# A four-layer graph network: own values summed by TensorE in the first convolution, first columns of the search placed ahead, and the last chunk of the edge stage divided

## The chip, the cores and the metric

The kernel runs on one core of one Trainium2 chip. A core has TensorE (PE, matrix multiplication, with a separate record for the loading of weights, PEld), VectorE (DVE), ScalarE (ACT), GpSimd (POOL, which here issues the indirect gathers) and SyncE (SP, which here issues the plain DMAs). [...] The metric is the device time of one execution in microseconds, median over runs.

## The reference, cut to what matters

A graph of 6250 nodes with 64 features and 206,250 directed edges (every edge both ways, and a loop at each node), sorted by destination. Four residual layers, each on the normalised and clipped values:

```python
h = jnp.maximum(_layernorm(x, axis=-1), 0.0)
x = x + _L0_gnn_ref(h, edge_index, W3, b3, W4, b4)      # two convolutions, A + an extra loop
h = jnp.maximum(_layernorm(x, axis=-1), 0.0)
x = x + _L1_gnn_ref(h, edge_index)                      # one pass of the normalised A
h = jnp.maximum(_layernorm(x, axis=-1), 0.0)
x = x + _L2_gnn_ref(h, edge_attr_64, src, dst, ...)     # an edge network, mean of squares by node
h = jnp.maximum(_layernorm(x, axis=-1), 0.0)
x = x + _L3_gnn_ref(edge_index, h)                      # three passes, mean of four embeddings
...
# _L0: y = D^-1/2 (A + I) D^-1/2 x, then W and b; a relu between the two
# _L2: msg = sigmoid(x @ Bw + Bb) * Vp[src] + (x @ Cw + Cb); M = clip(msg, EPS)^2, mean over dst, root
# _L3: embs = A (norm[row] * norm[col] * embs), three times; (emb + embs1 + embs2 + embs3) / 4
```

The self loop that the convolution adds on top of the loops of the graph is the `+ I` of L0: each node's own value is added to what it gathers. In the last layer, the first of the three passes needs the output of the edge layer at every node.

## The kernel before, in words

**Layout.** Nodes are padded to 49 blocks of 128 (6272). Seven chunks of seven blocks (`CB`) are 896 nodes (`W`); fourteen strips of 448 nodes (`CW`). The kernel builds the dense matrix of edge counts, A, in fp8, strip by strip of 448 columns, and stores it in DRAM as seven arrays of 128 x 49 x 896; all passes are then matmuls with that matrix. fp32 node values are split into three bf16 parts that add up to them (`split`, L709 to L715: ACT rounds, DVE subtracts, ACT rounds, DVE subtracts) and kept as `U3` or `V3`: 128 nodes x 49 blocks x 3 parts x 64 features. A pass multiplies all three parts. There are two forms of it. In `spread` (L742 to L750) the values are the weights and the matrix the moving operand, 448 wide: features come out on the partitions, with the parts going to two halves that are added when turned to nodes (`to_nodes`, L735 to L740, seven fp32 matmuls with a doubled identity `twice`). In `gather` (L1002 to L1031) pieces of the matrix (784 KB, 7 x 7 blocks) are the weights and the values move, 192 wide (3 parts x 64): an output chunk takes 343 matmuls in four PSUM banks `p_acc`, opened by four matmuls with a tile of zeros; four DVE reduces add the three parts, and the function `then` takes the chunk on.

**Stage 1, 0 to 166 us.** Inputs, the normalised values H0, and a search for where each block of 256 matrix columns begins in the edge list. For 25 columns DVE counts in a table `near` how many entries lie below the column's start (L801 to L804); one scaling (L805) and one conversion to integers (L806) follow for all 25, and POOL then gathers for each column, with these as indices, a stretch of the list (`near2`, L869) and with a second, exact index the run of edges (`run`, L878). The first strip is built here; degrees and U3 follow.

**Stage 2, to 563 us.** Fourteen strips; each has fourteen steps of `build` (DVE compares two digits with a count, L849; PE multiplies, L858; ACT writes the strip, L862). Beside the building of one strip `convolve` multiplies the one before (`spread` for 49 blocks, in fourteen stretches), and `hidden` takes a whole chunk through the two dense layers of L0: it turns the sum to nodes, copies it (ACT, L951), adds the three parts of the own values with three DVE adds (`add_whole`, L717 to L723), scales it (L954), multiplies, and splits the result into V3.

**Stages 3 and 4, to 1058 us.** Two gathers, for the second convolution (`convolved`; the seventh chunk's `hidden` and the constants of the edge stage, `prepared`, are taken in steps between its pieces) and for L1 (`turned`).

**Stage 5, to 3662 us: edges.** 202 groups of 1024 edges go through 208 slots as a pipeline seven slots deep (`slot`, an order written out by hand for PE, ACT and DVE). In each slot one group is fetched (eight indirect DMAs of POOL, L1325), others are in the edge network, gated (L1356, L1360 to L1362), squared and summed to nodes. When the groups of a chunk of nodes are through, `finished` (L1293 to L1304) takes the root, adds to X, normalises and splits the chunk into the U3 of the last layer. Beside that, a list `todo` is worked off, some items in each slot. It holds loads of pieces (SP, L1226), comparisons of A with its transpose that verify the edge list (`crossed`: PE turns four or three blocks, L1234, DVE compares, L1240), and the parts of the first pass of the last layer (`partial`: for chunk i, once it is finished, its 21 matmuls of 448 for one strip, L1252, which DVE adds to `Y`, L1258). The planner takes in slot i the number of open items divided by the slots left to the next deadline; the deadlines `ends` (L1308, L1315) are the slots in which the seven chunks end: 35, 64, 93, 122, 151, 180, 207. The last chunk ends with the last slot, so its part of the first pass is left for the next stage.

**Stage 6, to the end: three passes of L3.** In the first (L1498 to L1511) the last chunk's part is done: seven pieces, fourteen strips of 21 matmuls, DVE adds each to `Y` (L1509), and for every second strip `to_nodes` and `propagated` (L1477 to L1495: scale, scale again, `split` into the next pass's V3, and add to H). The second and third passes are gathers. PE, DVE and ACT have no order written out by hand here; the second pass's first matmul comes after the first pass's last. The functions touched stand below, with the lines of the profile.

Of the kernel before, what the change touches and what calls it, by code (L numbers as in the profile page):

```python
# [16 lines left out]
P = 128  # L17
# [578 lines left out]
QN = 32  # L596
DRIFT = 32
# [19 lines left out]
def fast(ctx, tc, bad, x, src, dst, edge_attr, W3, b3, W4, b4, w1, b1, w2, b2, Bw, Bb, Cw, Cb,  # L617
# [47 lines left out]

    node = ctx.enter_context(tc.tile_pool(name="node", bufs=1, reuse_waits="tile"))
# [24 lines left out]
    def normed(h, X_c):  # L691

        m = stat.tile([P, CB], F32, name="m")
        nc.vector.tensor_reduce(m, X_c, axis=AX.X, op=OP.add)
        nc.vector.tensor_scalar_mul(m, m, 1.0 / D)
        nc.vector.tensor_sub(h, X_c, over_features(m))
        q = stat.tile([P, CB, D], F32, name="q")
        nc.vector.tensor_mul(q, h, h)
        v = stat.tile([P, CB], F32, name="v")
# [3 lines left out]
        nc.vector.scalar_tensor_tensor(h, h, 0.0, over_features(v), op0=OP.max, op1=OP.mult)  # L703
# [4 lines left out]

    def split(u, U3, c):  # L709
        u3 = U3[:, blocks(c), :, :]  # L710
        nc.scalar.activation(u3[:, :, 0, :], u, AF.Copy)
        r = stat.tile([P, CB, D], F32, name="r")
        nc.vector.tensor_sub(r, u, u3[:, :, 0, :])
        nc.scalar.activation(u3[:, :, 1, :], r, AF.Copy)
        nc.vector.tensor_sub(u3[:, :, 2, :], r, u3[:, :, 1, :])  # L715
# [40 lines left out]
    with ExitStack() as ph:  # L756
# [44 lines left out]
        for c in range(GC):  # L801
            w = min(max(int(c * 2 * P * E / N / LOOK) - 22, 0), NS - SW)
            nc.vector.tensor_scalar(junk, near[:, w:w + SW], start_of[:, c:c + 1], float(w - 1),
                                    op0=OP.is_lt, op1=OP.add, accum_out=begin[:, c:c + 1])  # L804
        nc.vector.tensor_scalar(begin, begin, float(LOOK), 0.0, op0=OP.mult, op1=OP.max)  # L805
        nc.vector.tensor_copy(begin_i, begin)  # L806
# [20 lines left out]
        with ExitStack() as ps:  # L827
# [101 lines left out]
            for c in range(NC):  # L929
                u = wpool.tile([P, CB, D], F32, name="z", bufs=2)  # L930
                nc.vector.tensor_mul(u, H0[:, blocks(c), :], over_features(norm0[:, blocks(c)]))
                split(u, U3, c)
# [4 lines left out]
            def convolve(s, strip):  # L937

                p = psum.tile([P, 512], F32, name="p_sum", bufs=2)
                for q in range(NQ):  # L940
                    for b in range(q * NB // NQ, (q + 1) * NB // NQ):
                        spread(p, U3, b, strip[:, b, :], CW)
# [5 lines left out]
            def hidden(c, wpool, psum):  # L948

                z = wpool.tile([P, CB, D], F32, name="z", bufs=2)  # L950
                nc.scalar.activation(z, to_nodes(psum, y[c], CB), AF.Copy)  # L951
                yield
                add_whole(z, U3, c)
                nc.vector.tensor_mul(z, z, over_features(norm0[:, blocks(c)]))  # L954
# [16 lines left out]
                split(u, V3, c)  # L971
# [24 lines left out]
    def normed_and_split(h, U3, c, scale):  # L996
        normed(h, X[:, blocks(c), :])
        u = stat.tile([P, CB, D], F32, name="u")
        nc.vector.tensor_mul(u, h, over_features(scale[:, blocks(c)]))
        split(u, U3, c)  # L1000
# [554 lines left out]
```

## Time and profile before

| what | value |
| --- | --- |
| median of three runs | 4117.7 us (4096.95 to 4123.5) |
| profiled execution | 4134.23 us, span 4132.5 us |
| PE busy | 3161.0 us, 76% |
| DVE busy | 1984.4 us, 48% |
| ACT busy | 1257.3 us, 30% |
| POOL busy | 1663.9 us, 40% |
| edge stage | 1058 to 3662 us, granted TensorE clock 0.78 |
| rest of the first pass | 3673 to 3718 us |
| two later passes | 14 chunks of 28.95 us |

The page's groups name a line, an engine, an operation, the tiles written and read, and the count; after the bar stand the busy time, the mean duration of one in ns, and the idle time of the engine ahead of it with what ended that. Matmuls are pipelined and their ends are modelled, so a busy PE need not be at its peak. The waits name the engine and line that waited, what released it, the total, the number of times and the longest.

### The profile page before, as it was taken

To read this page: it belongs to the slowest core of one execution; us is meant where nothing else is said; L and a number is where in the kernel's file an instruction comes from. 1 tells how busy PE (TensorE), PEld (TensorE's weight loads), DVE (VectorE), ACT (ScalarE), POOL (GpSimd) and SP (SyncE) were. 2 spreads that over 40 slices of the span, in tenths; PEclk is the share of its full clock that TensorE was granted. 3 is DMA by queue.
4 is the path that set the end of the run, shared out by engine and by line. 5 is a ranking of instruction groups with operands and counts; after the bars stand their busy time and mean duration, and the time that the engine had idled before them with its cause. 6 is when DMAs were issued, how large, how long until landed. Compare 5 with 4: busy or idle time off the path is not lost.

```text
span 4132.5 us, 59248 instructions
## 1 busy us (share of the span) xinstructions
PE 3161.0 (76%) x24225; PEld 2164.1 (52%) x24225; DVE 1984.4 (48%) x3916; ACT 1257.3 (30%) x2031; POOL 1663.9 (40%) x1889
## 2 busy tenths in 40 slices
PE   1799999999566667676677667767767766689999
PEld 0566679998233334343334333334433433349999
DVE  6999945322245445454545443545544444461111
ACT  1577730000233333333333233333333333320000
POOL 4100010000566666656566656566666655600000
PEclk9799999999677767778787877777878777889999
DMA  3234355653322222222222222222222222136664
GB/s 99 74 83 109 85 167 188 204 179 117 97 66 60 46 56 72 56 82 56 65 66 64 62 66 62 65 63 60 81 57 73 68 53 68 45 106 194 196 203 151
DMA packets 229311, 388.75 MB, mean 94 GB/s; under 512 B 137573, under 2 KB 139743, under 8 KB 228771
## 3 DMA queue, kind: packets, MB, share of 16 engines
q1 hardware_dynamic: 170420, 321.51, 24.7%
q0 software_dynamic: 55104, 60.65, 7.7%
q8 instruction: 192, 3.15, 0.3%
q10 hardware_dynamic: 3504, 2.70, 0.3%
q14 instruction: 91, 0.75, 0.1%
HBM read 340.47 MB, written 44.24 MB: 93 GB/s over the span
## 4 chain that ended last, share of the span: by engine, by line
PE 51%; DVE 16%; another core or an unknown queue 13%; issue 9%; ACT 7%; DMA 2%; POOL 1%; DVEq 0%; SPq 0%; ACTq 0%; POOLq 0%
PE p_acc L1017 18%; PE p_sum L748 9%; PE p_bc L1351 7%; PE p L1337 5%; PE p_a L858 3%; DVE junk L1240 2%; ACT h L1341 2%; PE p_s L1379 2%; DVE m L1361 2%; DVE m L1360 2%; PE p_bc L1347 2%; PE p_e L1333 2%; DVE m L1362 1%; ACT gate L1356 1%
## 5 line engine op out<-in xcount | busy, mean ns | idle before, releaser
L1325 POOL DMA_INDIRECT v<-Vp_dram,src_g x1616 | 1590.6, 984 | 1348.6 <-issue 818.9
L1017 PE MATMUL p_acc<-U,piece 128*128 128x192 bf16 x9604 | 818.1, 246 | 3.6 <-DMA piece<-A 3.6
L1017 PEld LDWEIGHTS <-piece 128*128 128x128 fp8e4 x9604 | 799.1, 98 | 15.8 <-issue 4.7
L1351 PE MATMUL p_bc<-BC,h 128*128 128x256 f32 x1616 | 572.9, 486 | 6.9 <-issue 6.3
L1234 PE MATMUL p_sum<-ident_b,piece 128*128 128x128 bf16 x1372 | 160.1, 240 | 369.6 <-DVE junk L1240 325.2
L1360 DVE TENSOR_TENSOR m<-gate,v 128x512 f32<-128x512 f32 x202 | 140.1, 693 | 626.9 <-ACT gate L1356 417.4
L1240 DVE SCALAR_TENSOR_TENSOR junk<-p_sum,there 128x512 bf16<-128x512 f32 (+1 forms) x392 | 242.0, 617 | 394.7 <-remote 307.5
L1351 PEld LDWEIGHTS p_bc<-BC,h 128*128 128x128 f32 x1616 | 336.0, 231 | 163.4 <-issue 127.2
L1234 PEld LDWEIGHTS <-piece 128*128 128x128 fp8e4 x1372 | 120.6, 109 | 527.0 <-issue 505.6
L748 PEld LDWEIGHTS <-U 128*64 128x64 bf16 x4116 | 234.3, 113 | 303.5 <-issue 167.2
L862 ACT ACTIVATE strip<-p_a 128x784 fp8e4<-128x784 f32 x392 | 302.0, 820 | 118.6 <-PE p_a L858 102.6
L748 PE MATMUL p_sum<-piece,U 128*64 128x448 fp8e4 x2058 | 272.4, 384 | 80.9 <-issue 59.6
L1337 PE MATMUL p<-h,w_d 128*128 128x512 f32 x404 | 270.0, 752 | 73.6 <-ACT h L1341 58.8
L1027 DVE TENSOR_REDUCE zg<-p_acc 128x128 f32<-128x384 f32 x112 | 56.9, 508 | 534.8 <-PE p_acc L1017 534.1
L1341 ACT ACTIVATE h<-p,b_c 128x512 f32<-128x512 f32 x404 | 261.3, 685 | 169.0 <-remote 80.6
L1424 ACT ACTIVATE m<-m 128x512 bf16<-128x512 f32 x202 | 127.3, 630 | 594.0 <-DVE m L1423 468.6
L1379 PE MATMUL p_s<-m,to 128*128 128x192 bf16 x1616 | 207.0, 276 | 117.9 <-DVE r_s L1387 61.7
L1347 PE MATMUL p_bc<-BC_b,ones 3*128 3x512 bf16 x404 | 181.9, 450 | 118.8 <-DVE m L1361 105.3
L1337 PE MATMUL p<-eT,w_d 128*128 128x512 f32 x404 | 250.2, 705 | 17.7 <-issue 8.1
L1367 ACT ACTIVATE m<-m 128x512 bf16<-128x512 f32 x202 | 127.2, 630 | 431.0 <-DVE m L1362 342.8
L1379 PEld LDWEIGHTS <-to 128*128 128x128 bf16 x1616 | 174.1, 150 | 145.3 <-issue 141.3
L1347 PEld LDWEIGHTS <-ones 3*128 3x128 bf16 x404 | 37.5, 93 | 399.5 <-issue 208.2
(198 smaller groups left out, 3488.8 us busy)
## 6 DMA issues: line engine op xcount, KB each, us to landing
piece<-A SPq DMA_DIRECT2D x249, 784.0 KB
e<-in_edge_attr SPq DMA_DIRECT2D x202, 256.0 KB
A<-strip SPq DMA_DIRECT2D x14, 2744.0 KB
v<-Vp_dram,src_g POOLq DMA_INDIRECT x1616
there<-A SPq DMA_DIRECT2D x28, 784.0 KB
pairs<-pair SPq DMA_DIRECT2D x1, 1616.0 KB
Vp_dram<-v SPq DMA_DIRECT2D x7, 224.0 KB
out<-X SPq DMA_DIRECT2D x6, 224.0 KB
```

The source lines that it names most:

```text
L748: nc.tensor.matmul(p[half * D:(half + 1) * D, :w], U3[:, b, k, :], at_block, start=(i < 2), stop=(i >= 3 * n - 2))
L862: nc.scalar.activation(strips[s][:, :, col:col + 2 * SG].rearrange("p b (j l) -> p b j l", l=2), p[:, :, :2 * NB].rearrange("p j (b l) -> ...
L1017: nc.tensor.matmul(p[d // 2][:, d % 2 * 3 * D:(d % 2 + 1) * 3 * D], t[:, b, d * P:(d + 1) * P], U3[:, k * CB + b, :, :].rearrange("p t f - ...
L1234: nc.tensor.matmul(p[:, a - a0, :], held["here"][:, a, b * P:(b + 1) * P], ident_b, start=True, stop=True)
L1240: nc.vector.scalar_tensor_tensor(junk[:, :(a1 - a0) * P], p[:, :a1 - a0, :].rearrange("p a q -> p (a q)"), 15.5, there, op0=OP.min, op1=OP ...
L1325: nc.gpsimd.indirect_dma_start(out=v[:, j, :], out_offset=None, in_=Vp_dram[:, :], in_offset=bass.IndirectOffsetOnAxis(ap=src_g[:, g, j:j ...
L1337: nc.tensor.matmul(of[g][p], w, of[g].pop(x), start=True, stop=True)
L1341: nc.scalar.activation(of[g][t], of[g].pop(p), **how)
L1347: nc.tensor.matmul(p_bc[:, 4 * b:4 * b + 4].rearrange("p j o f -> p (j o f)"), ones, BC_b, start=True, stop=False)
L1351: nc.tensor.matmul(p_bc[:, 2 * q:2 * q + 2].rearrange("p j o f -> p (j o f)"), h2[:, q * P:(q + 1) * P], BC, start=False, stop=(k == 1))
L1360: nc.vector.tensor_mul(m, of[g].pop("gate"), of[g].pop("v"))
L1379: nc.tensor.matmul(p, to[:, :, j], m3[:, j].rearrange("p t f -> p (t f)"), start=(j == 0), stop=(j == J - 1))
```

## The change

Five edits.

1. In the search the 25 columns go in three groups (0 to 2, 3 to 9, 10 to 24); each group's scaling and conversion follow its own columns.
2. In `convolve` PE adds the own values: ahead of the last block's matmuls of a strip, twelve matmuls take U3's parts of the strip's own nodes with columns of the identity into the same bank. `hidden` then has no copy and no `add_whole`: the scaling reads PSUM.
3. The tile of zeros is made once, ahead of everything, and `gather` has a parameter for the steps taken beside it.
4. The edge stage knows eight parts in place of seven chunks (`PARTS`): the last chunk is divided in its first four blocks and its last three (`LATE`). The deadlines are 35, 64, 93, 122, 151, 180, 196 and 207. When the four blocks are finished, their loads (seven, of 448 KB) and sums (fourteen, of 12 matmuls) are put on the list, and between them `by_node` turns each finished chunk of `Y` to nodes (seven matmuls, and a copy to `Yn`).
5. The last three blocks' part of the first pass is in the gather's form: seven chunks of 21 matmuls of 192 columns in four banks `p_late`, four reduces, the addition of `Yn`, and `propagated`. It is a generator, `rest_of_first`: two chunks go ahead, and the others between the pieces of the second pass's first output chunk. The order of PE and DVE in this stage is now as written.

```diff
-        for c in range(GC):
...
-        nc.vector.tensor_scalar(begin, begin, float(LOOK), 0.0, op0=OP.mult, op1=OP.max)
-        nc.vector.tensor_copy(begin_i, begin)
+        for c0, c1 in ((0, 3), (3, 10), (10, GC)):
+            for c in range(c0, c1):
...
+            nc.vector.tensor_scalar(begin[:, c0:c1], begin[:, c0:c1], float(LOOK), 0.0,
+                                    op0=OP.mult, op1=OP.max)
+            nc.vector.tensor_copy(begin_i[:, c0:c1], begin[:, c0:c1])
...
                     for b in range(q * NB // NQ, (q + 1) * NB // NQ):
+                        if b == NB - 1:
+                            for d in range(s * CW // P, -(-(s + 1) * CW // P)):
+                                lo_, hi_ = max(d * P, s * CW), min((d + 1) * P, (s + 1) * CW)
+                                for k in range(3):
+                                    nc.tensor.matmul(
+                                        p[k % 2 * D:(k % 2 + 1) * D, lo_ - s * CW:hi_ - s * CW],
+                                        U3[:, d, k, :], ident_b[:, lo_ - d * P:hi_ - d * P],
+                                        start=False, stop=False)
                         spread(p, U3, b, strip[:, b, :], CW)
...
-                nc.scalar.activation(z, to_nodes(psum, y[c], CB), AF.Copy)
-                yield
-                add_whole(z, U3, c)
-                nc.vector.tensor_mul(z, z, over_features(norm0[:, blocks(c)]))
+                nc.vector.tensor_mul(z, to_nodes(psum, y[c], CB),
+                                     over_features(norm0[:, blocks(c)]))
...
+        PARTS = [(c * CB, CB) for c in range(NC - 1)] + [(NB - CB, CB - LATE), (NB - LATE, LATE)]
...
+        def by_node(k):
+
+            p = ps_a.tile([P, 512], F32, name="p_sum", bufs=2)[:, :CB * D].rearrange(
+                "p (b f) -> p b f", f=D)
+            y = Y[:, 2 * k:2 * k + 2, :].rearrange("p s w -> p (s w)")
+            for b in range(CB):
+                nc.tensor.matmul(p[:, b, :], y[:, b * P:(b + 1) * P], twice, start=True, stop=True)
+
+            def copied():
+                nc.vector.tensor_copy(Yn[:, blocks(k), :], p)
+
+            return copied
...
-            if c < NC - 1:
-                plan(CROSS[c], True)
+            if part < NC - 1:
+                plan(CROSS[part], True)
+            elif part == NC - 1:
+                for k in range(NC):
+                    todo.append((piece, lo, n, k))
+                    todo.append((partial, part, 2 * k))
+                    if k:
+                        todo.append((by_node, k - 1))
+                    todo.append((partial, part, 2 * k + 1))
+                todo.append((by_node, NC - 1))
...
-        ends = [last[c * CB + CB - 1] for c in range(NC)]
+        ends = [last[lo + n - 1] for lo, n in PARTS]
...
-                for s in range(CS):
-                    if s % 2 == 0:
-                        whole = apool.tile([P, CB, W], COUNT, name="piece")
-                        nc.sync.dma_start(whole, A[s // 2][:, blocks(NC - 1), :])
-                    t = whole[:, :, s % 2 * CW:(s % 2 + 1) * CW]
-                    p = psum.tile([P, 512], F32, name="p_sum", bufs=2)
-                    for b in range(CB):
-                        spread(p, U3, NB - CB + b, t[:, b, :], CW, NB - CB, CB)
-                    nc.vector.tensor_add(Y[:, s, :], Y[:, s, :], p[:, :CW])
-                    if s % 2:
-                        propagated(s // 2, to_nodes(
-                            psum, Y[:, s - 1:s + 1, :].rearrange("p s w -> p (s w)"), CB))
...
+        def rest_of_first():
+
+            for c in range(NC):
+                t = apool.tile([P, LATE, W], COUNT, name="late", bufs=NC)
+                nc.sync.dma_start(t, A[c][:, NB - LATE:, :])
+                p = [psum.tile([P, 512], F32, name=f"p_late{q}") for q in range(4)]
+                for d in range(CB):
+                    for b in range(LATE):
+                        nc.tensor.matmul(
+                            p[d // 2][:, d % 2 * 3 * D:(d % 2 + 1) * 3 * D],
+                            t[:, b, d * P:(d + 1) * P],
+                            U3[:, NB - LATE + b, :, :].rearrange("p t f -> p (t f)"),
+                            start=(b == 0), stop=(b == LATE - 1))
+                z = wpool.tile([P, CB, D], F32, name="zg")
+                summed_parts(z, p)
+                nc.vector.tensor_add(z, z, Yn[:, blocks(c), :])
+                propagated(c, z, V3)
+                yield
+
+        with tc.manual_schedule(engines={ET.PE, ET.DVE}):
+            rest = rest_of_first()
+            next(rest)
+            next(rest)
+            gather(apool, wpool, psum, V3, to_last, rest)
+            gather(apool, wpool, psum, values[0], to_out)
```

The diff's remaining lines give `normed`, `split` and `normed_and_split` a stretch of blocks in place of a chunk's number, and move the reduces of `gather` into `summed_parts`.

## The prediction

> **What bounds the kernel now.** I read the share of each engine by stage first. The columns are length, PE, weight load, DVE, ACT and POOL busy, granted TensorE clock, DMA share and GB/s. The stages in order: the strips of A, the edge stage, the step from it to the last passes, the rest of the first pass, and the first output chunk of the second pass.
>
> ```profile
> 166.00:563.00 397.00, 394.62 (x4899) 255.91 (x4901) 381.99 (x408) 294.93 (x409) 0.05 (x1) 1.00 0.32 87
> 1058.00:3662.00 2604.00, 1802.77 (x8343) 1000.06 (x8343) 1224.32 (x2713) 866.26 (x1448) 1580.99 (x1606) 0.78 0.25 65
> 3662.00:3674.00 12.00, 3.84 (x26) 1.71 (x24) 9.12 (x21) 2.03 (x4) 0.00 (x0) 0.73 0.01 1
> 3674.00:3718.00 44.00, 44.00 (x383) 27.71 (x380) 26.52 (x45) 6.92 (x12) 0.00 (x0) 0.96 0.35 111
> 3718.00:3748.00 30.00, 30.00 (x359) 29.68 (x358) 4.76 (x9) 1.15 (x2) 0.00 (x0) 1.00 0.59 189
> ```
>
> The reader sees three regimes: two full engines in the strips, no full engine in the edge stage (63% of the span), and PE alone from 3674 on. The groups of the strips, by shape, tell which of PE and DVE leads there:
>
> ```profile
> L849 DVE TENSOR_TENSOR lo<-count,key 128x2048 bf16<-128x2048 bf16 x172 | 209.6, 1219 | 0.0
> L849 DVE TENSOR_TENSOR hd<-turns,key 128x1568 bf16<-128x1568 bf16 x171 | 165.7, 969 | 8.1 <-PE p_a L858 7.3
> L858 PEld LDWEIGHTS <-lo 128*128 128x128 bf16 x2752 | 134.1, 98 | 65.2 <-DVE lo L849 44.8 <-issue 11.9 <-DVE hd L849 4.2
> L723 DVE TENSOR_TENSOR z<-z,r 128x448 f32<-128x448 f32 x6 | 3.7, 618 | 0.8 <-ACT z L951 0.8
> ```
>
> PE's weight loads wait 49 us for DVE, DVE waits 7 us for PE: DVE leads. In the edge stage the waits are a circle:
>
> ```profile
> POOL v L1325 <- DVE m L1360: 503.1, 91, 13.9
> ACT m L1424 <- DVE m L1423: 468.6, 141, 18.3
> PE p_sum L1234 <- DVE junk L1240: 325.2, 90, 13.0
> ```
>
> POOL's gathers of v, eight at about 1.25 us, fill 10 us of a mean slot of 12.74 us. Last, the tail from 3663 to 3748:
>
> ```profile
> L748 PE MATMUL p_sum<-piece,U 128*64 128x448 fp8e4 x304 | 35.9, 372 | 8.2 <-ACT U L711 7.4 <-ACT U L714 0.7
> L739 PE MATMUL p_node<-twice,Y 128*128 128x64 f32 x98 | 13.8, 281 | 0.0
> L1509 DVE TENSOR_TENSOR Y<-Y,p_sum 128x448 f32<-128x448 f32 x14 | 8.7, 619 | 5.5 <-PE p_sum L748 5.1
> L713 DVE TENSOR_TENSOR r<-u,U 128x448 f32<-128x448 f32 x8 | 5.0, 625 | 1.5 <-ACT U L711 0.8
> L714 ACT ACTIVATE U<-r 128x448 bf16<-128x448 f32 x8 | 4.6, 577 | 5.5 <-DVE r L713 5.5
> L1027 DVE TENSOR_REDUCE zg<-p_acc 128x128 f32<-128x384 f32 (+1 forms) x4 | 2.0, 508 | 23.0 <-PE p_acc L1017 23.0
> ```
>
> PE waits 8 us for U3 and is then never idle. The start of the program is a chain, whose POOL waits for begin_i:
>
> ```profile
> L869 POOL DMA_INDIRECT near<-pairs,begin_i x25 | 26.6, 1065 | 51.9 <-DVE begin_i L806 44.0 <-issue 6.1 <-DVE exact_i L875 0.6
> ```
>
> [...] granted clock 0.5 from 3667.5 to 3677.7, after the wait for U3. [...] An output chunk of the later passes takes 28.95 us for 347 matmuls here, 83.4 each.
>
> **The change, part by part.**
>
> *First columns ahead.* The near gather (L869) starts at 48.58, after the scale and cast (0.18 each) of all 25 columns. Placing three columns first would let it start near 40.3. But in the order of the changed program the first gather's wait is still on the count of the last column's search: its tile takes the space of the searched one, which must be read to the end. It saves two small operations ahead of the wait and adds four: 4 x 0.18 - 0.36, **+0.3**. If the wait were on the first group alone: -3.7.
>
> *Own values by TensorE.* For each of six chunks in the strips DVE loses three adds (0.610 + 0.616 + 0.618 = 1.84 us), ACT a copy (0.55); the scaling reads PSUM instead. Two strips take 62.9 us, of which 28 builds are 57.1, so what DVE drops is nearly all time: about 1.6 x 6 = -9.7. PE gains 12 matmuls of up to 128 columns for each strip[...], hidden by PE's slack of 0.36 us for each build (14 in a strip). The last strip's stand before the first piece of gather 1, which waits for its DMA until 580.67 though p_sum ended at 576.85. I take **-8**; ends: -11 (all DVE time) and +6 (PE leads[...]). The zeros tile made once: nothing on the path.
>
> *Edge stage.* Planned items are spread over slots, with a deadline when a chunk ends. The six block-row chunks before keep their deadlines. The last is divided: its first four blocks end in slot 196, three in 207. So the planned work of slots 181 to 207 (about three items in each) is now in 181 to 196 (five). An item's price: the mean slot is 12.09 us in the first chunk (1.55 crossings in each slot) and 12.90 in the sixth (1.93 crossings, 0.48 sums). That and a fit over all slots bracket 0.4 to 0.64 for a crossing and 0.93 to 1.84 for a sum of 21 matmuls. Added: 14 sums of 12 matmuls (12/21 of 0.96, 0.55) and 7 turns to nodes (0.6). Eight sums of 21 leave the last five slots (26 us, PE-led: 8 x 2.27 = 18.2 us); 5 small sums and 3 turns (9.2 us) take their place: I take -7 of the 9, as the slot's own chain is late next. Earlier slots get those eight (8 x 0.93 = 7.4) and the other nine sums and four turns (7.4). Finishing four blocks amid the stage: the five slots that finish a chunk take 18.8 us, six over the mean; with smaller operations 5. Sum 7.4 + 7.4 - 7 + 5 = **+13**. [...] Crowding therefore goes up to +45. Below zero: -8, where circle waits (POOL's 503 us) swallow the items and only the lighter last slots count.
>
> *Step to the last passes.* From the last slot to U3 is 11.1 us (3662.5 to 3673.6); 15 operations shrink from 448 to 192 columns: [...]**-3.7**. A last copy to Yn: **+0.6**.
>
> *Rest of the first pass.* Before: PE starts 3673.0, the second pass's first chunk ends 3747.67, 74.6 us. Removed: 14 x 21 matmuls of 448 columns (2.2 us a strip), 49 turns and the 14 Y adds. Added: seven chunks of 21 matmuls of 192 columns (21 x 83.4 ns = 1.75 us), between pieces (49 x 83.4 = 4.1). PE's step is 5.85 us. DVE's chain for a chunk, in the written order: four reduces 2.0, Yn 0.62, z 0.64, u 0.62, wait for ACT 0.73, r 0.63, wait 0.64, U 0.62, H 0.62: 7.15. A piece waits for its chunk's U, so **DVE becomes the bound**: the first late bank 0.5, seven chains 50, the last piece 4.1 and its tail 1: 55.6, so -19. The first matmuls are at half clock: +1.5. **-17.5**; ends -27 (PE's 5.85 a step) and -10 (chain 8 us). Late pieces are 336 KB, seven of them with seven whole ones are 7.8 MB in 55 us, 143 GB/s, under the 189 of the later passes. Later passes keep their work.
>
> Sum: 0.3 - 8 + 13 - 3.7 + 0.6 - 17.5 = **-15.3**. Against the profiled execution (4134.23 around a span of 4132.5) that is 4119; it lies 16.5 above the median of the runs shown, so from 4117.7 I get **4102**.
>
> **Rivals.**
> - *Crowding (slower).* Slots 181 to 196 hold five items and feed SP's queue; if the bound there is the items' own chain, each grows by 2 to 4 us, the stage by 30 to 60. From +28 on the whole is slower than before; at +45 it gives 4134. For it: slots of 25 us recur where crossings are three to a slot. Against: mean slots barely follow the items.
> - *PE-bound tail.* DVE's chain overlaps more than I allow, and the items are free: -8 - 3.1 - 27 + 3 = -35, 4083. Against: two ACT waits stand in the written order.
> - *No effect ahead.* The columns placed first do not start POOL earlier: that is in my forecast; were it otherwise, 4099.
> - *Strips turn PE-bound.* +6 in place of -8: 4116. For it: PE is shown 99% busy, though its ends are modelled.
>
> **How the numbers follow.** Forecast and its neighbour 4099: 0.52. Strips: 0.13. PE-bound tail: 0.17. Crowding: 0.18. About 1%, 41 us, is what a measurement of this kernel can tell (the three runs spread by 26.5). Faster than 4076.5 needs the tail and more: 0.1. Slower than 4159 needs crowding beyond +70: 0.09. Range: 4076 to 4140, from the PE-bound tail with some spread to crowding at +45 with the runs' own spread.
>
> **What would show it.** POOL's first gather still near 48.9; two strips in 61.2 us; the sixth chunk's slots 181 to 196 about 14 us; first late matmul about 8 us after the last slot; seven DVE chains 7.1 us apart with PE waiting for U between pieces; the second pass's first chunk ending 56 us after that matmul. Wrong if slots 181 to 196 pass 16 us, or if PE never waits there.

## The result and the profile after

The changed kernel takes 4122.9 us (median of 20 runs), the kernel before 4119.98 (20 runs): ratio 0.9996, 95% interval 0.9976 to 1.0015. Nothing has moved that can be measured. The ratio rests on the fast runs alone (one of the changed kernel's twenty, 4164.44 us, is counted as slow), so it is not the quotient of the two medians. The forecast was 15 us less.

The two profiled executions are 24 us apart (4110.15 against 4134.23), and that must not be read as the result: runs of one kernel spread over 60 to 77 us, and in the traces nearly all of the spread is in the edge stage. What repeats from trace to trace is the rest of the program. So I read the two traces by part, and for the edge stage take three traces of each kernel (the second and third come from the experiments, same kernels, with slots of the same length):

| part | predicted | measured | from |
| --- | --- | --- | --- |
| start and strips, to the start of the last build | -7.7 | +2.6, +3.0, +3.3 | 559.2 to 561.8; 559.7 to 562.7; 559.3 to 562.6 |
| edge stage, its last 25 slots (from slot 180 to 205) | +13 | +23 | 317.8, 315.5, 307.6 before; 327.1, 346.2, 337.1 after |
| from the last addition of edges to the first reduce of the second pass | -20.6 | -26.8 | 84.6, 84.7, 85.0 before; 57.8, 57.7, 58.3 after |

Between the second row and the third, up to the last addition of edges, another 1 to 2 us go. The sum is about +1, and the measured ratio says -1.6 (-10 to +6). The 176 earlier slots of the edge stage hold the same items in both kernels and differ only by their spread (2215 to 2250 us before, 2233 to 2262 after). So a saving of 27 us in the tail is there, the strips lost 3 in place of giving 8, and the end of the edge stage gave the rest back.

**Strips.** Groups by shape in the strips, after:

```profile
L856 DVE TENSOR_TENSOR lo<-count,key 128x2048 bf16<-128x2048 bf16 x172 | 209.0, 1215 | 0.0
L856 DVE TENSOR_TENSOR hd<-turns,key 128x1568 bf16<-128x1568 bf16 x171 | 165.2, 966 | 19.4 <-PE p_a L865 17.9
L865 PEld LDWEIGHTS <-lo 128*128 128x128 bf16 x2736 | 133.6, 98 | 59.7 <-DVE lo L856 37.0 <-issue 14.6 <-DVE hd L856 4.7
```

The three adds are gone, and DVE's idle time ahead of hd has grown from 8.1 to 19.4 us: the 11 us that were freed became a wait for PE. Why is seen when the stage is cut at its strips and not averaged. First a strip without dense layers beside it, then one with them (the columns are those of the stages in the prediction); before:

```profile
309.70:338.00 28.30, 27.98 (x374) 17.90 (x370) 28.30 (x29) 21.98 (x30) 0.00 (x0) 1.00 0.37 101
338.00:372.60 34.60, 34.56 (x417) 22.75 (x413) 32.50 (x36) 25.29 (x37) 0.00 (x0) 1.00 0.31 83
```

and after:

```profile
310.30:338.60 28.30, 28.30 (x383) 18.45 (x380) 28.30 (x29) 21.86 (x30) 0.00 (x0) 1.00 0.37 101
338.60:373.70 35.10, 34.89 (x431) 23.36 (x428) 31.05 (x33) 24.91 (x36) 0.00 (x0) 1.00 0.30 82
```

A plain strip is VectorE's: 28.30 busy of 28.30. A strip with the dense layers was PE's already before: VectorE has 32.50 busy of 34.60, PE 34.56. The change takes VectorE's work out of just these strips (31.05 busy now) and puts matmuls into them: 35.1.

**Edge stage.** Waits, after:

```profile
POOL v L1368 <- DVE m L1403: 524.5, 94, 15.7
ACT m L1468 <- DVE m L1467: 438.4, 134, 20.6
DVE junk L1260 <- remote: 287.0, 39, 17.7
```

The same circle as before ("remote" is a releaser that the profile cannot name; the kernel before has 307.5 us of it at its comparisons too). The planned work is where the prediction put it: in slots 181 to 196 PE starts 916 matmuls, 645 before. The last 25 slots take 13.5 us each in place of 12.5. A finer cut tells more: slots 181 to 196 take 225.7, 234.7 and 235.3 us (205.5, 198.7 and 208.2 before), and from there to the last addition of edges it is 89.2, 90.5 and 92.2 (100.1, 95.0 and 87.2 before). The crowded slots lost 28 us, and the lighter ones behind them gave back 3 or 4.

**Tail.** One chunk of VectorE's chain, the second of the seven, in order of time:

```profile
3679.47 1.74 DVE L1019 TENSOR_REDUCE zg<-p_late 128x128 f32<-128x384 f32 x4
3681.24 0.62 DVE L1564 TENSOR_TENSOR zg<-zg,Yn 128x448 f32<-128x448 f32 x1
3681.90 0.62 DVE L1524 TENSOR_TENSOR z<-zg,norm 128x448 f32<-128x448 f32 x1
3682.56 0.62 DVE L1527 TENSOR_TENSOR u<-z,norm 128x448 f32<-128x448 f32 x1
3683.83 0.62 DVE L717 TENSOR_TENSOR r<-u,U 128x448 f32<-128x448 f32 x1 [0.64 <-ACT U L715]
3685.09 0.62 DVE L719 TENSOR_TENSOR U<-r,U 128x448 bf16<-128x448 f32 x1 [0.64 <-ACT U L718]
3685.64 0.62 DVE L1530 TENSOR_TENSOR H<-H,z 128x448 f32<-128x448 f32 x1
3686.17 1.74 DVE L1019 TENSOR_REDUCE zg<-p_late 128x128 f32<-128x384 f32 x4
```

The chain takes 6.70 us (3679.47 to 3686.17), with both waits for ScalarE in it (the first chunk takes 7.8, waiting for PE at its reduces), and PE waits for it, as the groups from 3658 to 3735 show:

```profile
L1037 PE MATMUL p_acc<-U,piece 128*128 128x192 bf16 x477 | 41.6, 246 | 9.0 <-DVE U L719 9.0
L1557 PE MATMUL p_late<-U,late 128*128 128x192 bf16 x147 | 14.7, 263 | 5.3 <-DVE U L719 5.3
```

**Start.** POOL still waits for the end of the search. The releaser shown is now the scaling of the last group, which ends at 48.00 us, and no longer begin_i:

```profile
L876 POOL DMA_INDIRECT near<-pairs,begin_i x25 | 26.0, 1042 | 51.9 <-DVE begin L811 43.5 <-issue 5.5 <-DVE digits L889 1.6
```

The first gather starts at 48.09 us (48.58 before).

### The profile page after: what moved, and what is told of

Its sections match the earlier page's. It is cut to its first block, busy times and chain, and to the rows that moved or that the text cites. A ratio compares the mean times of both kernels' runs of the same rounds, so it can differ in the third digit from the quotient of the medians.

```text
span 4108.0 us, 59675 instructions
## 1 busy us (share of the span) xinstructions
PE 3144.2 (77%) x24414; PEld 2172.4 (53%) x24414; DVE 1995.9 (49%) x3952; ACT 1257.5 (31%) x2030; POOL 1659.2 (40%) x1889
## 4 chain that ended last, share of the span: by engine, by line
PE 52%; DVE 16%; another core or an unknown queue 12%; issue 9%; ACT 7%; DMA 2%; POOL 0%; DVEq 0%; ACTq 0%; SPq 0%; POOLq 0%
PE p_acc L1037 17%; PE p_sum L752 10%; PE p_bc L1394 7%; PE p L1380 5%; PE p_a L865 4%; ACT h L1384 2%; PE p_s L1422 2%; DVE junk L1260 2%; DVE m L1404 2%; DVE m L1403 2%; PE p_bc L1390 2%; PE p_e L1376 1%; PE p_sum L1254 1%; DVE m L1405 1%
## 5 line engine op out<-in xcount | busy, mean ns | idle before, releaser
L1368 POOL DMA_INDIRECT v<-Vp_dram,src_g x1616 | 1586.0, 981 | 1368.8 <-DVE m L1403 524.5
L1394 PE MATMUL p_bc<-BC,h 128*128 128x256 f32 x1616 | 562.9, 478 | 14.2 <-issue 13.6
L752 PEld LDWEIGHTS <-U 128*64 128x64 bf16 x3990 | 234.1, 115 | 337.1 <-issue 208.1
L1380 PE MATMUL p<-h,w_d 128*128 128x512 f32 x404 | 260.3, 727 | 68.8 <-ACT h L1384 50.7
L1422 PE MATMUL p_s<-m,to 128*128 128x192 bf16 x1616 | 206.2, 276 | 90.5 <-DVE r_s L1430 44.0
L1380 PE MATMUL p<-eT,w_d 128*128 128x512 f32 x404 | 243.6, 687 | 14.6 <-ACT h L1384 10.4
L752 PE MATMUL p_sum<-strip,U 128*64 128x448 fp8e4 x2058 | 242.1, 359 | 2.5 <-ACT U L715 1.4
```

What stands on the lines that cost most here:

```text
L752: nc.tensor.matmul(p[half * D:(half + 1) * D, :w], U3[:, b, k, :], at_block, start=(i < 2), stop=(i >= 3 * n - 2))
L1368: nc.gpsimd.indirect_dma_start(out=v[:, j, :], out_offset=None, in_=Vp_dram[:, :], in_offset=bass.IndirectOffsetOnAxis(ap=src_g[:, g, j:j ...
L1380: nc.tensor.matmul(of[g][p], w, of[g].pop(x), start=True, stop=True)
L1394: nc.tensor.matmul(p_bc[:, 2 * q:2 * q + 2].rearrange("p j o f -> p (j o f)"), h2[:, q * P:(q + 1) * P], BC, start=False, stop=(k == 1))
L1422: nc.tensor.matmul(p, to[:, :, j], m3[:, j].rearrange("p t f -> p (t f)"), start=(j == 0), stop=(j == J - 1))
```

## The experiments

The experiments fell on three chips. On one of them the kernel before takes 4092 to 4182 us, with one run of 4215, much as in the result. On the two others it takes 3616, some 500 us less, and the traces put some 490 of these into the edge stage: 2065 to 2083 us from its first to its last comparison of nodes in the kernels traced there, 10.3 a slot, against 2523 to 2609 and 12.6 to 13.0. I call the first a long-slot chip and the others short-slot chips. The waits of the edge stage on a short-slot chip, in the kernel h_early below:

```profile
DVE m L1404 <- DMA v<-Vp_dram,src_g: 578.5, 144, 8.2
POOL v L1369 <- issue: 457.4, 1501, 0.3
PEld L1255 <- issue: 276.7, 432, 9.3
```

VectorE waits there for POOL's gathers; POOL's own waits for VectorE are too short in sum for such a list (in no_own, from 1100 to 3100 us, it goes down to 153.3 us without them). On the long-slot chip POOL waits 503.1 us (before) and 524.5 us (after) for VectorE. The strips have the same length on both kinds to 0.1 us and the tail to 2; the start of the program is some 5 us shorter on the short-slot chips. Ratios are always to the kernel before on the same chip; runs given without a ratio are single ones.

**The strips: without the own values (no_own)**

```diff
-                        if b == NB - 1:
-                            for d in range(s * CW // P, -(-(s + 1) * CW // P)):
...
```

> The changed kernel without the 168 own-value matmuls of the first convolution (the own values are left out of that layer's sum). Theory A: in the six strips that have dense layers beside them PE leads, so VectorE's dropped adds give nothing, and the own-value matmuls cost their 0.5 to 0.7 us a strip. Then a strip with dense layers takes 34.4 to 34.6 us (35.05 in the changed kernel, 34.6 before) and the last build starts near 559. Theory B: VectorE leads there as the prediction had it, and the own-value matmuls alone ate the gain. Then such a strip takes about 33.0 us and the last build starts near 550.

Measured on a short-slot chip: last build at 553.6, against 556.7 in a kernel with the changed strips on the same chip (h_early). The same two strips:

```profile
304.50:332.80 28.30, 28.10 (x375) 17.93 (x373) 28.30 (x29) 22.02 (x30) 0.00 (x0) 1.00 0.37 101
332.80:367.30 34.50, 34.27 (x415) 22.74 (x412) 30.95 (x33) 24.79 (x36) 0.00 (x0) 1.00 0.31 84
```

The dense strip falls to 34.5, the length before, though VectorE has 1.5 us less to do than before. Theory A holds: VectorE's adds were worth nothing there, and the own values cost 0.6 us in each of the six dense strips, which is the +3.

**The strips: own values three times (own_thrice)**

```diff
-                                for k in range(3):
+                                for k in (0, 1, 2) * 3:
```

> The changed kernel with the own-value matmuls made three times (36 for each strip; the own value is added three times). Theory: PE has only about 1.4 us to spare in a plain strip, of which the change takes 0.7; then a plain strip goes from 28.3 to about 29 us and one with dense layers from 35.05 to 36.2 or more. Rival (the prediction's step: 0.36 us to spare for each build, 5 us a strip): a plain strip stays at 28.3.

```profile
308.80:337.20 28.40, 28.40 (x392) 18.57 (x389) 28.32 (x29) 21.57 (x29) 0.00 (x0) 1.00 0.37 101
337.20:373.70 36.50, 36.29 (x464) 24.74 (x464) 31.15 (x33) 25.11 (x37) 0.00 (x0) 1.00 0.29 79
```

Half of what I expected fell. A plain strip takes 24 more matmuls for 0.1 to 0.2 us. A dense strip grows by 1.4 us: 24 matmuls cost that much where nothing hides them. So PE has at least 2 us to spare in a plain strip, an estimate from those 1.4 for 24 matmuls and the strip's 36; whether it has the whole 5 of the prediction is not shown. The slack was true in one kind of strip, and the saving lay in the other.

**The strips: dense layers spread over two (hidden_wide)**

```diff
                     for steps in beside * (2 if s == 1 else 1):
                         next(steps, None)
-                for steps in beside:
+                    if q % 4 == 1:
+                        for steps in slow:
+                            next(steps, None)
+                for steps in beside + (slow if s % 2 == 0 or s == CS - 1 else []):
...
-                    beside.append(hidden(s // 2 - 1, wpool, psum))
+                    slow = [hidden(s // 2 - 1, wpool, psum)]
```

> The changed kernel with the dense layers of a chunk spread over two strips in place of the first half of one. Theory A (PE leads only where they are crowded): a pair of strips falls from 63.4 to 60 to 61 us (VectorE's own work is 57.1 + 4 x 0.54 = 59.3), the last build starts near 545 to 549. Theory B (each step of the dense layers costs a stall of its own, wherever it stands): a pair stays at 63 to 63.5.

A pair takes 63.8 us (240.1 to 303.9), the last build starts at 556.8, as without the edit. The hope that plain strips have room for half of the dense layers fell: both strips of a pair now take 31.6 to 32.2. Whether each step of the dense layers costs a stall, or PE is full once it has half of them, these runs don't tell.

**The tail: H added in the wait (h_early)**

```diff
                 nc.vector.tensor_mul(u, z, s3)
-                split(u, V3, blocks(c))
+                nc.scalar.activation(V3[:, blocks(c), 0, :], u, AF.Copy)
             h = H[:, blocks(c), :]
             nc.vector.tensor_add(h, h, z)
+            if V3 is not None:
+                split(u, V3, blocks(c), True)
...
```

`True` tells `split` that the first rounding has been made.

> The changed kernel with the addition to H put between u and the first subtraction of the split, so that VectorE does it while it waits for ScalarE. Theory: VectorE's chain of 6.71 us a chunk is the bound of the rest of the first pass; it becomes 6.17, and from the first late matmul to the first reduce of the second pass's first chunk takes 46.3 us in place of 50.1. Rival: PE and the cold clock are the bound there; the chain is 6.2 but the stretch stays within 1 us of 50.1.

```profile
3164.85 1.74 DVE L1020 TENSOR_REDUCE zg<-p_late 128x128 f32<-128x384 f32 x4
...
3168.48 0.62 DVE L1531 TENSOR_TENSOR H<-H,z 128x448 f32<-128x448 f32 x1
3169.20 0.62 DVE L718 TENSOR_TENSOR r<-u,U 128x448 f32<-128x448 f32 x1
3170.47 0.62 DVE L720 TENSOR_TENSOR U<-r,U 128x448 bf16<-128x448 f32 x1 [0.64 <-ACT U L719]
3171.01 1.48 DVE L1020 TENSOR_REDUCE zg<-p_late 128x128 f32<-128x384 f32 x3
```

The addition fills the first wait, the chain is 6.16 us, and from the first late matmul to the first reduce it takes 46.9 us (3150.29 to 3197.19) in place of 50.1 (no_own and near_apart, same chip). The cold clock of the rival is the granted 0.50 that the changed kernel's trace shows from 3667.10 to 3673.93 us. VectorE's chain is the bound of the rest of the first pass, as predicted.

**The start: the searched table apart (near_apart)**

```diff
+        rpool = ph.enter_context(tc.tile_pool(name="rpool", bufs=3, reuse_waits="tile"))
         looked = ExitStack()
         npool = looked.enter_context(tc.tile_pool(name="npool", bufs=1, reuse_waits="tile"))
...
         looked.close()
-        rpool = ph.enter_context(tc.tile_pool(name="rpool", bufs=3, reuse_waits="tile"))
```

> The changed kernel with the searched table in a place that the first gather's tile does not take. Theory: the reuse of that place was all that held POOL's first near gather; it starts near 40.5 in place of 48.1, the first run gather near 45.7 (53.3), and the second strip's first build about 4 us earlier (127.9, from 131.6). Rival: the chain of run gathers that follows is bound elsewhere (three buffers, the keys of each column), and the second strip starts less than 1 us earlier.

```profile
L876 POOL DMA_INDIRECT near<-pairs,begin_i x25 | 25.2, 1008 | 47.2 <-DVE begin_i L814 35.3 <-issue 5.2 <-DVE exact_i L882 5.0
```

The first gather starts at 39.84 us, the first group's columns being all it waits for; so the reuse of the table's place was what held it. The first gather of a run of edges moves by only 1.2 (52.2; 53.4 in no_own), a miss, yet the second strip starts at 121.4 in place of 124.4 (no_own, same chip): 3 us, most of the 3.7 that the prediction gave as the value of this edit had it worked.

**Both kernels again (before_again, after_again)**

> The kernel before, run beside the others. In the first four runs it took 3615.9 us where the profiled execution on record took 4134: the edge stage's slots were 10.3 us long, paced by POOL's gathers, in place of 12.7. If this chip is of that kind: about 3616, ratio 1, slots of 10.3 us and POOL without waits for VectorE. If it is of the first kind: about 4120 and slots of 12.7.

> The changed kernel. Theory: strips, step and tail have fixed lengths (+3, -4, -22 and a little at the start, together about -24 against before), and only the edge stage depends on the chip. Where its slots are paced by POOL (10.3 us) the added items are hidden, and the whole is 24 to 26 us faster (ratio 0.993). Where slots are 12.7 us long, crowding gives some 20 us back (ratio 0.9985 to 1.000). Rival: the gain in the tail is given back by the edge stage everywhere: ratio 0.999 to 1.000 on either.

This was the long-slot chip. The kernel before against itself: 0.9983 (0.9962 to 1.0005), which tells what such a comparison can resolve. The changed kernel: 1.0004 (0.9975 to 1.0033), 14 runs. As expected for long slots.

**Two crossings moved to the first slots (cross_moved)**

```diff
-                 ((4, 6), (4, 5), (4, 0), (4, 1)), ((5, 6), (5, 0), (5, 1), (5, 2)))
-        FIRST = ((3, 3), (4, 4), (5, 5), (6, 6))
+                 ((4, 6), (4, 5), (4, 0), (4, 1)), ((5, 6), (5, 0)))
+        FIRST = ((3, 3), (4, 4), (5, 5), (6, 6), (5, 1), (5, 2))
```

> The changed kernel with two of the last chunk's four crossings, 28 items and their loads, moved to the first 36 slots: 3.06 items a slot in slots 181 to 196 in place of 4.81, and 2.5 in place of 1.67 in the first 36. Crowding theory: where slots are 12.7 us, 10 to 20 us less than the changed kernel; where POOL paces the slots, within 3 us of it. Rival (an item costs the same wherever it stands): within 3 us of the changed kernel on either.

Long-slot chip: 0.9990 (0.9967 to 1.0014). The ratio doesn't separate it from the changed kernel; the medians of the same session, 4138.5 against 4159.9, lie further apart, so the whole is open. The slots do separate them: the last 25 take 319.5 us, against 327.1 to 346.2, and slots 181 to 196 take 216.1 (212.4 in divided_again, which has the same move), against 225.7 to 235.3. The first 31, which took the items, take 381.5, against 358.7 to 376.7 in the changed kernel and 374.6 to 378.8 in the kernel before (the same items give 371.0 in divided_again). So time goes where the items leave: 16 and 20 us for 28 comparisons, 0.56 to 0.70 each. What they cost where they arrive is lost in the spread, so this run does not tell whether an item costs more in a crowded slot than elsewhere.

**The last chunk whole (whole_last)**

```diff
-LATE = 3
+LATE = 7
...
-        PARTS = [(c * CB, CB) for c in range(NC - 1)] + [(NB - CB, CB - LATE), (NB - LATE, LATE)]
+        PARTS = [(c * CB, CB) for c in range(NC)]
...
+                    if i == NC - 2:
+                        todo.append((by_node, k))
...
```

What is left out keeps the loads of the four blocks off the list, and gives `late` four buffers in place of seven.

> The changed kernel with its last chunk left whole: no deadline at slot 196, none of the 14 sums and 7 loads, the seven turns to nodes put with the sixth chunk's sums; the rest of the first pass takes 49 matmuls for each chunk in place of 21. Step to the last passes 3.7 longer again; PE's step in the tail is 8.2 us, so PE leads there and the tail grows by 8 to 11. Where POOL paces the slots: 10 to 15 us slower than the changed kernel. Where slots are 12.7: if crowding costs 20, 5 to 10 us faster than the changed kernel; if not, 10 to 15 slower.

Long-slot chip: 0.9933 (0.9901 to 0.9964), faster than both kernels, though its tail is 12 us longer than the changed kernel's (from the last addition of edges to the first reduce 70.1, PE's step of 8.1 leading). The last 25 slots take 318.6. So without the division the end of the edge stage is about as before, and what is left of the tail's gain counts. By its parts (strips +3, tail -14.6) the kernel would be 12 us faster, 0.997, so that a part of the 0.9933 is chance or not understood.

**Twice as crowded (crowded)**

```diff
-LATE = 3
+LATE = 5
...
```

The line left out gives `late` four buffers in place of seven.

> The changed kernel with the last chunk divided in two and five blocks: the deadline is slot 188, so the same 77 items stand in 8 slots (9.6 a slot) in place of 16. Tail and step to it are 5 to 7 us longer than the changed kernel's (35 matmuls a chunk, 2.9 + 4.1 us of PE a step against VectorE's 6.7; wider operations). Crowding theory: slots 181 to 188 take 22 us and more and the later ones win back less than half, the edge stage is 30 to 60 us longer than the changed kernel's on either kind of chip. Rival (an item costs the same wherever it stands): edge stage within 5 us, the whole 2 to 10 us slower than the changed kernel.

Short-slot chip: 0.9979 (0.9968 to 0.9989). Tail 62.6, 4.9 longer. The edge stage is 2082.8, against 2071.1 to 2076.0 in five kernels with the changed kernel's division on such chips: about 10 longer, not 30. The rival (an item costs the same anywhere) gave at most 5. So crowding the same number of items costs something on a chip that POOL paces, in one trace and at a third of the size I gave it. Slots 181 to 188 take 14.5 us each in place of 22, and the nine after them 7.3: of the 34 us that the crowded slots lose (against 10.3 a slot) the later ones win back 27, not less than half.

**Versions that combine (undivided, divided)**

The first is whole_last with near_apart and the strips as before; the second is the changed kernel with cross_moved, h_early, near_apart and the strips as before.

> The kernel with the last chunk whole, the searched table apart from the first gather's tile, and the strips as before (own values added by VectorE). Sum by the runs so far: last chunk whole 0.9933, start -3, strips -3: ratio about 0.992 where slots are 12.7 us. Where POOL paces them: tail -14.6, start -3, edge +1 to +4: 0.996.

> The changed kernel with two crossings moved to the first slots, the addition to H put into the wait for ScalarE, the searched table apart, and the strips as before. Fixed parts: -3 at the start, -3 in the strips, -3.2 in the tail, against the changed kernel. Where slots are 12.7 us: ratio to before 0.993 to 0.998, by how much the moved items relieve the edge stage. Where POOL paces them: 0.9905 (25 + 9 us of 3616).

Short-slot chip: undivided 0.9959 (0.9946 to 0.9973), as expected; divided 0.9887 (0.9872 to 0.9903), somewhat better than the 0.9905 expected.

**The open question on the long-slot chip (before_third, after_third, divided_again, undivided_again)**

> The kernel before, for its trace. If POOL paces the slots here: edge stage 2066 to 2072 us from the first to the last comparison of nodes, 3616 in all; if not, 2560 to 2570 and about 4130.

> The changed kernel. Where POOL paces the slots: its fixed parts alone decide (start -0.5, strips +3, step and tail -27) and the edge stage adds 2 to 4: ratio 0.993 to 0.994. Where slots are 12.7 us: 0.9975 to 1.001 as in the runs so far, the edge stage giving 20 to 25 back.

> The changed kernel with two crossings moved to the first slots, the addition to H in the wait for ScalarE, the searched table apart and the strips as before. Where POOL paces the slots: 0.9887 as measured. Where slots are 12.7 us: 0.995 if the moved items relieve the edge stage by some 10 us, 0.9975 if not at all (fixed parts -9 against the changed kernel).

> The kernel with the last chunk whole, the searched table apart and the strips as before. Where POOL paces the slots: 0.996 as measured. Where slots are 12.7 us: 0.992 (0.9933 for the whole last chunk alone, and -6 of fixed parts); if the 0.9933 was a chance of that comparison, 0.995 to 0.996 (its fixed parts are -21).

It was the long-slot chip again. The kernel before took 4097.3 in its one run, its edge stage 2522.7. The changed kernel: 0.9989 (0.9966 to 1.0013), again no difference. Divided: 0.9961 (0.9932 to 0.9989), undivided: 0.9955 (0.9930 to 0.9980). Both beat the kernel before, neither beats the other on this chip, and their intervals overlap the changed kernel's. Undivided has what its parts give (start and strips -5, tail -14). Divided does not: its parts give -34, the whole -16 (-28 to -4), so its edge stage still gives 6 to 30 us back, although its last 25 slots are as before; where, the spread hides.

The end of the edge stage in every trace. Slots are counted from the start of the comparison of nodes in each; the last column runs from slot 197 to the last addition of edges:

| chip and kernel | last 25 slots | slots 181 to 196 | behind them |
| --- | --- | --- | --- |
| long, as before | 317.8, 315.5, 307.6 | 205.5, 198.7, 208.2 | 100.1, 95.0, 87.2 |
| long, changed | 327.1, 346.2, 337.1 | 225.7, 234.7, 235.3 | 89.2, 90.5, 92.2 |
| long, two crossings moved | 319.5, 313.9 | 216.1, 212.4 | 93.4, 89.9 |
| long, last chunk whole | 318.6, 298.6 | 210.9, 196.4 | 96.3, 95.3 |
| short, changed (five kernels) | 261.1 to 263.8 | 168.7 to 172.2 | 80.6 to 84.0 |
| short, two crossings moved | 258.1 | 160.5 | 90.0 |
| short, last chunk whole | 256.5 | 156.9 | 96.1 |
| short, crowded | 276.4 | 174.2 | 88.7 |

On the long-slot chip the division costs some 23 us of slots. On a short-slot chip it costs next to nothing: against the one trace with the last chunk whole, slots 181 to 196 lose some 14 us, and what comes behind them gains 12 to 16. The changed kernel itself was not run on a short-slot chip; the four that differ from it by one small edit and were run beside the kernel before there took 3587 to 3593 against 3616, one run each, so that it would be some 25 us (0.7%) faster, which its fixed parts also give (+3 and -27). The kernel before was not traced there.

## Why the prediction was wrong

- **Strips, -8: wrong, +3 with the start in it.** The step that failed: "Two strips take 62.9 us, of which 28 builds are 57.1, so what DVE drops is nearly all time." A pair was averaged that is two regimes: VectorE full in the plain strip, PE in the dense one. The dropped work was all in the second (no_own: 34.5 us without the adds and without the own values, 34.6 before). That the own values are "hidden by PE's slack of 0.36 us for each build" failed there too: they cost 0.6 us in each dense strip (no_own) and nothing that shows in a plain one (own_thrice). That is 11 of the some 14 us between forecast and result. The rival that PE leads, put at +6 (the author's estimate) and 0.13, was the right one.
- **Edge stage, +13: right in kind, too small on the long-slot chip.** The last 25 slots grew by 23. The ratio, less strips and tail, leaves +22 (+14 to +30), within the range given for the stage (-8 to +45, the upper end the author's estimate). The term of the sum that was mis-sized is the price of the work in the crowded slots, with "Earlier slots get those eight (8 x 0.93 = 7.4)" and 5 for finishing four blocks. Slots 181 to 196 were put at about 14 us each and took 14.1 to 14.7 (12.4 to 13.0 before), +28 together where 14 makes +20; and the slots behind them gave back 3 or 4 in place of 7. The spread of three traces is as large as these differences, so the split is rough. Why the price was higher stays open. Without the division it is gone (whole_last); crowded shows on a short-slot chip that density alone costs something; on the long-slot chip 28 comparisons cost 0.56 to 0.70 us each where they left, at the top of the prediction's own 0.4 to 0.64, and density and number of items were not told apart. Nor were the seven loads in SP's queue tried apart from the items; that loads of pieces hold up the loads of e is not shown, and PE waits for the rows of e once in the kernel before, 5.8 us, and never in the changed one.
- **Step and tail, -20.6: right mechanism, -26.8.** VectorE is the bound, PE waits for U between pieces, and the rest of the pass lies within the ends given (-22 between -27 and -10). The chain measured 6.70 in place of 7.15 (the parts listed there add up to 7.12; its four reduces take 1.74 together in place of 2.0), 3 us over seven chunks. From the first late matmul to the end of the first output chunk it was 52.7 in place of 57.1. The half clock cost what was put for it: 0.50 is granted from 3667.10 to 3673.93 (before, from 3667.48, within PE's wait for U, to 3677.72), the first bank is reduced 1.15 us after the first matmul and the first chain is 1.07 longer than the others, 2.2 us in place of 0.5 and 1.5. The last piece with its tail took 3.6 in place of 5.1, beside the end of the last chain. The way from the last addition of edges to where the matmuls of the pass run on shrank by 4.9 (12.5 to 7.7) in place of 3.1 (the author's estimate); its additions and products took 0.62 us each at 448 columns and take 0.36 at 192. Before, one matmul stood alone at 3671.73, ahead of the 3673.0 that the prediction took for the start. The last copy to Yn came behind the last U and cost nothing.
- **Start, +0.3: -0.5 for the first gather.** A wait for the end of the search was foreseen and is there; near_apart shows the cause.
- The whole: 15 us faster was forecast, none is measured: +11 in the strips and +10 in the edge stage against -6 in the tail. That the time lies in the range owes something to luck, since the tail's gain hides part of the two misses; the sign was not earned on this chip.

## What to carry to other kernels

Cut a stage at its own period before asking which engine leads: a mean over two kinds of strip showed VectorE ahead, and the operations removed were all in the kind where PE led. Work moved to an earlier deadline is not moved for nothing even when the total stays (10 us in crowded): compare the items per slot with what slots of that density take. And when runs of a kernel spread by more than the change, compare parts of traces that repeat, and several traces of the part that doesn't.

## What I had not expected of the hardware

The kernel before took about 3616 us on two chips and 4090 to 4182, with one run of 4215, where slots are long. POOL's gathers were issued 1.25 us apart on all of them, and loads of e reached their last packet 2.3 to 2.4 us after issue on both kinds. Nor is 12.7 us the length of a slot: in the kernel before 73 of 201 take less than 9 us and 37 more than 18, often in turns of 7, 7 and 22. In h_early, on a short-slot chip, 144 take 9 to 12.

What differs in the traces is PE: where slots are long there are stretches in which its instructions start on a grid of 0.70 us, one or more steps apart, with no wait shown. Matmuls of the crossings in the kernel before:

```profile
3574.88 0.27 PE L1234 MATMUL p_sum<-ident_b,piece 128*128 128x128 bf16 x1 [0.77 <-issue]
3576.97 0.27 PE L1234 MATMUL p_sum<-ident_b,piece 128*128 128x128 bf16 x1 [1.82 <-issue]
3577.67 0.29 PE L1234 MATMUL p_sum<-ident_b,piece 128*128 128x128 bf16 x1 [0.44 <-issue]
3579.07 0.27 PE L1234 MATMUL p_sum<-ident_b,piece 128*128 128x128 bf16 x1 [1.11 <-issue]
```

Runs of three and more such starts (one to three steps apart, to 0.03 us) add up to 57 to 88 us in each of the ten traces with long slots, and to none in the eight with short ones. The waits of the other engines say the same more loudly. VectorE's comparisons in the edge stage, first in the kernel before, then in h_early:

```profile
DVE junk L1240 <- remote: 307.5, 39, 16.3
DVE junk L1261 <- PE p_sum L1255: 19.7, 20, 3.5
```

In the ten traces with long slots VectorE waits 398 to 522 us and ScalarE 286 to 464 us between the first and the last comparison of nodes for such a "remote" release; in the eight others neither does at all. The semaphore is in every case one that PE's instructions raise, and it comes long after the ends that the profile models for them: in the kernel before by 5.2 us in the middle and 13.5 at most for VectorE's waits, 3.2 and 11.7 for ScalarE's. VectorE's idle time there is 1256 to 1325 us against 799 to 814, a difference as large as that of the stage. The granted clock is lower too (0.78 against 0.86 in the stage); whether that is cause or result is not shown. So the longer slots go with PE's signals coming late. What makes them late is not shown. The packets of the queue that the page calls instruction took as long on both kinds (16 KB, 0.97 to 1.06 us in the middle). Each run on record has a granted clock beside its time, so none tells whether the stretches are there without the profiler.
